# Own step lists for the first units, one more pair of half 0 before half 1, and residual updates moved behind the mixers

## The chip, the cores and the metric

The kernel runs on one core of a Trainium2 chip. The core has five engines with a queue of instructions each: TensorE (PE in the profile) for matrix products and transposes, VectorE (DVE) and GpSimd (POOL) for elementwise work, ScalarE (ACT) for activations and copies, and SyncE (SP), which here only issues DMAs. Each engine works through its own queue in order and waits on semaphores for the others. Matrix results go to PSUM, everything else lies in SBUF. The metric is the device time of one execution in microseconds (us).

## The reference, cut to what matters

There are 1024 tokens (4 sequences of 256) of 512 fp32 values, and two layers of two blocks each. Each block reads a normalised copy of the residual stream and adds its result to it:

```
x = hidden_states                                    # 4 x 256 x 512, fp32
# block 1: retention, 32 query heads, 8 key/value heads, head size 128
y  = layernorm(x)
q, k = rope(y Wq), rope(y Wk);  v = y Wv;  g = y Wg
dt = softplus(y Win + bias);  a = cumsum(-exp(A) * dt)
x += (rmsnorm(causal(exp(a_i - a_j) * q k^T) v) * silu(g)) Wo
# block 2: router, 64 experts, the best 8, and a bias for each expert
# block 3: state space, 128 heads of 64 channels, 8 groups
xs, B, C = silu(conv4(y Wx)), silu(conv4(y WB)), silu(conv4(y WC))
h = causal(exp(a_i - a_j) * C B^T) (dt * xs) + D * xs
x += (rmsnorm per group (h * silu(y Wz))) Wout       # groups of 1024 channels
# block 4: 64 adapters of rank 16, the best 16
```

## The kernel before, in words

**Tiling.** The 1024 tokens are 8 tiles of 128 rows, in two halves of 4 tiles (two sequences each, 512 tokens, the free size of most matmuls). The residual `k.x[t]` stays in SBUF as fp32. An fp32 product is made of three matmuls of split operands: a high part `hi` and the rest `lo`, so hi·hi, lo·hi and hi·lo. Normalised activations lie transposed in `k.xs[half]` as a hi and a lo part. `normalize` (its first part is `moments`, L86: `bn_stats` of each tile) writes them: hi by ACT (L126), lo by DVE (L127).

**Weights.** A weight comes in pieces of 128x1024 (512 KB). `Weights` keeps all pieces in the order of their use. `until(n)` loads every piece up to number n, splits it in `split` (hi is a copy on ACT, L140; lo a subtraction on POOL, L145), and issues the loads of the two pieces after it. A step W calls `step`, which splits the next piece only if its number is at most `due`; `due` is -1 until block 3 runs, so W does nothing in block 1. A piece that nobody asked for earlier is split at its first use. For the numbers in `LATE`, ACT's copy keeps the place it has in the program.

**Order of the work.** Instructions are not sent in the order in which the functions emit them: a scheduler plays the program through on a timeline with its own costs and orders each engine's queue by that. `k.behind(one, made, ...)` adds a dependence without a semaphore's cause in the data: `one` has to be placed behind `made`. The order of emission is written in lists of single letters, one list for each unit of work.

**Block 1** goes through 32 units (key/value head, pair of query heads, half). While unit i is attended, the projections of unit i+1 are emitted: S are the scores q k^T (L408), A the products with v (L420) and the norms, Q the query projection, K the steps of keys and values, G the gate projection, U the silu of the gate, N the norm and the cast to yh (L451) and yl (L452), F and C the output product with Wo (L464) of the unit before, D the decays (`exponents`, up to L303: the row of cumulated sums comes back from DRAM by a broadcast DMA `gb`, is added to the column on DVE and POOL in L299, masked in L303 and goes through exp on ACT). The first unit has the list FIRST1, the others of the first part STEP1. `queries` and `keys` go through `rope` (L355 to L365): two products on DVE, a sum on POOL, a hi copy on ACT and a lo subtraction on DVE (L365).

**Block 2** (router) and the preparation of blocks 3 and 4 are side work, `k.side`: generators from which a step P, T or E takes a piece while the main block goes on.

**Block 3** goes through 64 items: 8 groups of 4 channel pairs, twice, once for each half. For an item, X are the convolution's products and sums (L732), I its inputs, T the transposes (L796), M the mixer (m = decays times C B^T on DVE in L773, the products with it in L821, `xs += skip` in L831 on DVE, the gate in L835 on POOL, yh and yl in L839 and L840), O the output product of the item before (L877) and the sum over the pairs of a group into `acc` (L885), D the decays of the next item. The four settling operations of a group and half, `x += acc * r` (L891, 128x512), follow the output tiles of the group's last pair. `r` is the group's root mean square, of POOL (L863). The order of the items is set by `order`: a first range of pairs of half 0 and then the same pairs of half 1, then each pair for half 0 and half 1 in turn, and a last range of two. A pair that does half 1 straight behind half 0 uses the same split weights; in the first range the weights are loaded and split once for each half. `steps_of` makes the softplus and the cumulated sums of a half before its first item: `ps_v`, a chain of small DVE and ACT operations up to L251, then the products L255 (`ps_cum`), L264 (`ps_in`) and L273 (`ps_tail`).

Of the kernel before, what the change touches and what calls it, by code (L numbers as in the profile page):

```python
# [18 lines left out]
P = 128  # L19
# [8 lines left out]
LONE1, FIRST3, LONE3 = 3, 1, 2  # L28
# [3 lines left out]
LATE = (0, 3)  # L32
FIRST1 = "U S0 S1 S2 K Q0 W Q1 K A0 A1 W K G0 N0 W G1 N1 D E W".split()
STEP1 = "S0 D F S1 S2 K Q0 W Q1 K A0 A1 U W K C W P G0 N0 W G1 N1 E P W".split()
SIDE1 = "S0 D F P S1 S2 T K Q0 P W Q1 T K A0 A1 U W K C P P W G0 P N0 W G1 N1 E P W".split()
STEP3 = "W T0 T1 B I0 W M0 M1 X0 X1 I1 O0 G0 W W O1 W W P O2 W W G1 P W O3 D0 D1 W W".split()
# [3 lines left out]
SIDE3 = "T0 T1 I0 I1 M0 M1 P B X0 X1 P P O0 W O1 G0 G1 W W P O2 O3 W P W P D0 D1 E E".split()  # L40
# [41 lines left out]
def moments(k, tc, t, tag):  # L82

    nc = tc.nc
    stats = k.small([P, 6], f"stats_{tag}_{t}", "ln_stats")
    nc.vector.bn_stats(stats, k.x[t])  # L86
    mv = k.small([P, 2], f"mv_{tag}_{t}", "ln_mv", 6)
    nc.vector.bn_aggr(mv, stats)
    rstd = k.small([P, 1], f"rstd_{tag}_{t}", "ln_rstd", 6)
    nc.gpsimd.tensor_scalar_add(rstd, mv[:, 1:2], EPS)  # L90
    one = nc.gpsimd.tensor_tensor(rstd, rstd, k.neghalf[:, 0:1], ALU.pow)
    if tag == "4" and t == HT - 1:
        k.rooted = one
    return mv[:, 0:1], rstd
# [18 lines left out]
def normalize(k, tc, half, tag, into=("xn",)):  # L113


    nc = tc.nc
    tiles = [HT * half + at for at in range(HT)]
    of = [moments(k, tc, t, tag) for t in tiles]
    ahead = len(into)
    xns = [centre(k, tc, tiles[at], of[at], tag, into[at]) for at in range(ahead)]  # L120
    yield
    for at, t in enumerate(tiles):
        xn = xns[at]
        ps = turned(k, tc, xn, f"xn_{tag}_{t}")
        hi, lo = (part[:, :, at * P:at * P + P] for part in k.xs[half])
        nc.scalar.copy(hi, ps)  # L126
        nc.vector.tensor_tensor(lo, ps, hi.bitcast(F32), ALU.subtract)  # L127
        if at + ahead < HT:
            xns.append(centre(k, tc, tiles[at + ahead], of[at + ahead], tag, into[at % ahead]))
        yield  # L130
# [179 lines left out]
def retention(k, tc, io, arrive, begun, done, tail):  # L310
# [5 lines left out]
    with ExitStack() as st:  # L316
# [35 lines left out]
        def rope(ps, hi, lo, name):  # L352
# [3 lines left out]
            if name == "k_0_0":  # L356

                tc.keep_in_program_order(one)
            t2 = k.wk.tile([P, 2, SEQ], F32, tag="xd", name=f"r2_{name}")
# [5 lines left out]
            nc.vector.tensor_tensor(lo, t1, hi.bitcast(F32), ALU.subtract)  # L365
# [143 lines left out]
        for i in range(-1, len(units) + 1):  # L509
# [50 lines left out]
            def value(z):  # L560
# [9 lines left out]
                W=k.weights.step,  # L570
            )
# [100 lines left out]
def state_space(k, tc, io):  # L672
# [141 lines left out]
    def mixer(p, n):  # L814
# [16 lines left out]
        nc.vector.scalar_tensor_tensor(  # L831
            xs, xs, skip[:, ch:ch + 1], ps_y.rearrange("p t l -> p (t l)"),
            ALU.mult, ALU.add,
        )
        nc.gpsimd.tensor_tensor(xs, xs, p.sg[n], ALU.mult)  # L835
# [29 lines left out]
    def output(p, t):  # L865
# [20 lines left out]
        if p.cp == NC // 2 - 1 and p.g < NG - 1:  # L886
            settle(p, t)

    def settle(p, t):
        xt, a = k.x[HT * p.half + t], acc[p.g, p.half][:, t, :]  # L890
        one = nc.vector.scalar_tensor_tensor(xt, a, p.r[:, t:t + 1], xt, ALU.mult, ALU.add)  # L891
        if (p.g, p.half) == (NG - 1, 0):
            k.behind(one, own.made, "products first")

    cbs, sqs, acc = {}, {}, {}

    pairs, uses = [], []

    order = [range(FIRST3 * NC // 2)]
# [22 lines left out]
    def run(done):  # L922


        with tc.tile_pool(name="s3", bufs=1, reuse_waits="tile") as own.only:
            for i in range(-1, len(pairs) + 1):
# [207 lines left out]
def tile_two_layers(ctx: ExitStack, tc: tile.TileContext, io: dict, out: bass.AP):  # L1134
# [60 lines left out]
    k.hold = k.scaled = k.turned = None  # L1195
    k.const = ctx.enter_context(tc.tile_pool(name="const", bufs=1))
# [112 lines left out]
```

## Time and profile before

| quantity | value |
|---|---|
| median of three runs | 2538.18 us (2537.22 to 2538.46) |
| the profiled execution's own time | 2536.5 us |
| its span, first to last instruction | 2534.7 us |
| PE busy | 2425.6 us (96%), granted clock 0.987 of full speed |
| DVE / POOL / ACT busy | 2062.1 (81%) / 1597.8 (63%) / 1473.0 us (58%) |
| DMA | 206.25 MB, mean 81 GB/s |

Block 1 fills the span up to about 790 us, block 3 begins its products at about 860 us, the decays' steps of its half 1 lie at about 1020 to 1040 us, and the adapters take the last 100 us. In the page, a line of a group names the line of the code, the engine, the operation, output and input, the count, then the busy time and the mean of one, then the engine's idle time just before these instructions and what ended most of it. In a timeline a row has start, duration, engine, line, operation and shape; a bracket at its end is the engine's idle time before it, with the instruction that it waited for. PE's granted clock is 1.00 at full speed.

### The profile page before, as it was taken

To read this page: it belongs to the slowest core of one execution; us is meant where nothing else is said; L and a number is where in the kernel's file an instruction comes from. 1 tells how busy PE (TensorE), PEld (TensorE's weight loads), DVE (VectorE), ACT (ScalarE), POOL (GpSimd) and SP (SyncE) were. 2 spreads that over 40 slices of the span, in tenths; PEclk is the share of its full clock that TensorE was granted. 3 is DMA by queue.
4 is the path that set the end of the run, shared out by engine and by line. 5 is a ranking of instruction groups with operands and counts; after the bars stand their busy time and mean duration, and the time that the engine had idled before them with its cause. 6 is when DMAs were issued, how large, how long until landed. Compare 5 with 4: busy or idle time off the path is not lost.

```text
span 2534.7 us, 36875 instructions
## 1 busy us (share of the span) xinstructions
PE 2425.6 (96%) x14000; PEld 2008.6 (79%) x14000; DVE 2062.1 (81%) x2629; ACT 1473.0 (58%) x2363; POOL 1597.8 (63%) x1123
## 2 busy tenths in 40 slices
PE   7899999999999897899999999999999999999989
PEld 6688888888887775678878888888888888888767
DVE  6577677778888769697988988988988988979973
ACT  3555555556655455465766756666756657657631
POOL 4555546557766547485874865856756855857840
PEclk9899999999999998999999999999999999999999
DMA  3312212213332222332232323222323223323221
GB/s 108 77 58 67 57 44 67 68 50 100 92 92 63 88 77 69 96 117 76 84 92 69 107 67 92 92 76 84 100 67 100 84 67 96 95 69 108 82 90 69
DMA packets 82896, 206.25 MB, mean 81 GB/s; under 512 B 8672, under 2 KB 10592, under 8 KB 82720
## 3 DMA queue, kind: packets, MB, share of 16 engines
q1 hardware_dynamic: 82720, 203.90, 26.5%
q8 instruction: 111, 1.82, 0.3%
q14 instruction: 65, 0.53, 0.1%
HBM read 200.86 MB, written 3.01 MB: 80 GB/s over the span
## 4 chain that ended last, share of the span: by engine, by line
PE 37%; DVE 15%; POOL 6%; issue 4%; ACT 3%; DMA 1%; POOLq 0%; SPq 0%; ACTq 0%; DVEq 0%
PE ps_x L206 9%; PE ps_g L206 8%; PE ps_o L877 8%; DVE m L773 4%; PE ps_y L821 4%; DVE conv L732 3%; PE ps_bc L206 3%; DVE yl L840 2%; PE ps_o L1122 2%; POOL xs L835 1%; DVE m L299 1%; POOL sqs L849 1%; PE ps_t L796 1%; PE ps_h L206 1%; ACT m L1160 1%
## 5 line engine op out<-in xcount | busy, mean ns | idle before, releaser
L206 PE MATMUL ps_g<-xs_hi,wg_h 128*128 128x512 f32 x768 | 306.4, 399 | 2.3 <-ACT wg_h L140 1.7
L773 DVE TENSOR_TENSOR m<-m,cb 128x1536 f32<-128x1536 f32 x128 | 274.7, 2150 | 40.2 <-ACT m L1160 38.8
L206 PE MATMUL ps_g<-xs_lo,wg_h 128*128 128x512 f32 x768 | 300.1, 391 | 0.0
L206 PE MATMUL ps_g<-xs_hi,wg_l 128*128 128x512 f32 x768 | 298.6, 391 | 0.0
L732 DVE SCALAR_TENSOR_TENSOR conv<-ps_x,cw,conv 128x510 f32<-128x510 f32 (+2 forms) x384 | 269.9, 736 | 20.1 <-ACT conv L730 17.5
L1157 ACT ACT_TABLE_LOAD x191 | 245.1, 1283 | 4.1 <-PEq L1297 0.8
L299 POOL TENSOR_TENSOR m<-gb,start 128x512 f32<-128x512 f32 x128 | 151.4, 1185 | 140.6 <-PE ps_y L821 93.0
L877 PE MATMUL ps_o<-wo_h,yh 128*128 128x512 f32 x512 | 213.0, 416 | 20.0 <-DVE acc L885 18.9
L835 POOL TENSOR_TENSOR xs<-xs,sg 128x512 f32<-128x512 f32 x128 | 206.7, 1615 | 38.2 <-DVE xs L831 37.3
L849 POOL TENSOR_TENSOR sqs<-sqs,sq 128x512 f32<-128x512 f32 x112 | 192.9, 1722 | 32.9 <-ACT sq L847 32.9
L362 POOL TENSOR_TENSOR r_q<-r_q,r_q 128x512 f32<-128x512 f32 x64 | 103.3, 1613 | 175.0 <-DVE r_q L361 174.8
L303 POOL TENSOR_SCALAR_AFFINE_SELECT m<-m 128x1024 f32<-128x1024 f32 x160 | 206.0, 1287 | 0.1
L877 PE MATMUL ps_o<-wo_h,yl 128*128 128x512 f32 x512 | 198.2, 401 | 7.8 <-DVE yl L840 7.8
L1160 ACT ACTIVATE xs<-conv,cb 128x512 f32<-128x512 f32 x128 | 90.8, 723 | 193.2 <-DVE conv L732 193.1
L877 PE MATMUL ps_o<-wo_l,yh 128*128 128x512 f32 x512 | 202.7, 396 | 0.0
L206 PE MATMUL ps_x<-xs_lo,wx_h 128*128 128x512 f32 x512 | 202.6, 396 | 0.0
L206 PE MATMUL ps_x<-xs_hi,wx_h 128*128 128x512 f32 x512 | 202.0, 395 | 0.4 <-DVE conv L732 0.2
L206 PE MATMUL ps_x<-xs_hi,wx_l 128*128 128x512 f32 x512 | 201.3, 393 | 0.0
L1160 ACT ACTIVATE m<-m 128x1024 f32<-128x1024 f32 (+1 forms) x160 | 181.5, 1135 | 28.0 <-POOL m L303 28.0
L145 POOL TENSOR_TENSOR wo_l<-raw_wo,wo_h 128x1024 fp32r<-128x1024 f32 x60 | 147.8, 2464 | 79.1 <-ACT wo_h L140 71.8
L145 POOL TENSOR_TENSOR wx_l<-raw_wx,wx_h 128x1024 fp32r<-128x1024 f32 x38 | 96.3, 2534 | 154.3 <-ACT wx_h L140 141.5
L821 PE MATMUL ps_y<-m,xd 128*64 128x128 f32 x2048 | 178.1, 280 | 13.5 <-DVE m L773 9.5
(276 smaller groups left out, 6949.1 us busy)
## 6 DMA issues: line engine op xcount, KB each, us to landing
gb<-cum SPq DMA_DIRECT2D x160, 512.0 KB
raw_wx<-in_L_attn_in_x_dram SPq DMA_DIRECT2D x38, 512.0 KB
raw_wg<-in_L_attn_in_gate_dram SPq DMA_DIRECT2D x38, 512.0 KB
raw_wo<-n_L_attn_out_proj_w_dram SPq DMA_DIRECT2D x38, 512.0 KB
raw_wq<-in_L_attn_Wq_dram SPq DMA_DIRECT2D x22, 512.0 KB
raw_wg<-in_L_attn_Wg_dram SPq DMA_DIRECT2D x22, 512.0 KB
raw_wo<-in_L_attn_Wo_dram SPq DMA_DIRECT2D x22, 512.0 KB
raw_wkv<-in_L_kv_dram SPq DMA_DIRECT2D x11, 512.0 KB
```

What stands on the lines that cost most here:

```text
L145: low = nc.gpsimd.tensor_tensor(lo, w, hi.bitcast(F32), ALU.subtract)
L206: k.line(tc.nc.tensor.matmul(ps, a[:, c, :], b[:, c, :], start=(c == 0 and n == 0), stop=(c == KC - 1 and n == 2)))
L299: one = engine.tensor_tensor(m[:, blk], gb[:, min(blk, 1)], last(at, P), ALU.add)
L303: nc.gpsimd.affine_select(out=causal, in_=causal, compare_op=ALU.is_ge, fill=GONE, base=0, pattern=[[0, 8], [1, P]], channel_multiplier=-1,)
L732: nc.vector.scalar_tensor_tensor(acc[:, :, j:], ps[:, :, :SEQ - j], cw[:, ch, TAPS - 1 - j:TAPS - j], acc[:, :, j:], ALU.mult, ALU.add,)
L773: made = nc.vector.tensor_tensor(mh, mh, cbs[p.g, p.half].rearrange("p z b l -> p z (b l)").unsqueeze(2) .to_broadcast([P, 3, 2, 2 * P]), ...
L821: one = nc.tensor.matmul(ps_y[h * D:h * D + D, 2 * b + z, :], p.xe[:, n, b, h, :] if blk == 2 else xd[:, 2 * b + zs, h, :], m[:, blk, 2 * ...
L835: nc.gpsimd.tensor_tensor(xs, xs, p.sg[n], ALU.mult)
L849: nc.gpsimd.tensor_tensor(total, total, sq, ALU.add)
L877: own.out = nc.tensor.matmul(ps, y[:, at], w[:, n, :], start=(i == 0), stop=(i == 5))
L1157: load = nc.scalar.preload_act_table_set(table)
L1160: ins = nc.scalar.activation(out, in_, func, bias=bias, scale=scale)
```

## The change

- FIRST1 and STEP1 lose their W steps (which do nothing there). Both get a V, STEP1 also V1. V calls `weights.until` with a number: for the first unit (i = 0) that of its Wo piece (3, `wo1_0_0`), for the second (i = 1) 6 with V (`wo1_0_1`) and 7 with V1 (the kv piece of the fifth unit, `wkv1_1_0`), and -1, which asks for nothing, for every other unit. Piece 7 joins LATE.
- `moments`: the `bn_stats` of half 1 in block 1 are placed behind the lo part of the same tile of half 0 (`k.parts`).
- `rope`: the cosine product of the second part of the first keys (`k_0_1`) is placed behind the last lo subtraction that was made, that of the first queries (`k.low`).
- FIRST3 counts pairs instead of groups and goes from 4 pairs (one group) to 5. Half 0 does group 0 and the first pair of group 1, then half 1 the same; from there on the two halves take turns as before. One pair's weights (bc, x, g, o) are loaded and split a second time: 4 loads of 512 KB, 4 ACT copies (L140), 4 POOL subtractions (L145).
- The settling operations leave `output`. `ended`, now called by a step Z at the end of STEP3 and SIDE3 too, puts the four of a group and half into `own.late`; each `mixer` (two in an item) takes two of them behind its own L831. They are placed behind that L831 by `k.behind` (`own.made` is otherwise the newest product of L773). For the last group they are issued in `ended` as before. There are 64 of them before and after.

```
-LONE1, FIRST3, LONE3 = 3, 1, 2
+LONE1, FIRST3, LONE3 = 3, 5, 2
-LATE = (0, 3)
-FIRST1 = "U S0 S1 S2 K Q0 W Q1 K A0 A1 W K G0 N0 W G1 N1 D E W".split()
-STEP1 = "S0 D F S1 S2 K Q0 W Q1 K A0 A1 U W K C W P G0 N0 W G1 N1 E P W".split()
+LATE = (0, 3, 7)
+FIRST1 = "U S0 S1 S2 K Q0 Q1 K A0 A1 K V G0 N0 G1 N1 D E".split()
+STEP1 = "S0 D F S1 S2 K Q0 W Q1 K A0 A1 V U K C P G0 V1 N0 G1 N1 E P".split()
-STEP3 = "... G1 P W O3 D0 D1 W W".split()
+STEP3 = "... G1 P W O3 D0 D1 Z W W".split()
-SIDE3 = "... O2 O3 W P W P D0 D1 E E".split()
+SIDE3 = "... O2 O3 W P W P D0 D1 Z E E".split()
...
 def moments(k, tc, t, tag):
-    nc.vector.bn_stats(stats, k.x[t])
+    one = nc.vector.bn_stats(stats, k.x[t])
+    if tag == "1" and t >= HT:
+        k.behind(one, k.parts[t - HT], "half 0 first")
...
 def normalize(k, tc, half, tag, into=("xn",)):
-        nc.vector.tensor_tensor(lo, ps, hi.bitcast(F32), ALU.subtract)
+        k.parts[t] = nc.vector.tensor_tensor(lo, ps, hi.bitcast(F32), ALU.subtract)
...
     def rope(...):
+            if name == "k_0_1":
+                k.behind(one, k.low, "queries first")
...
-            nc.vector.tensor_tensor(lo, t1, hi.bitcast(F32), ALU.subtract)
+            k.low = nc.vector.tensor_tensor(lo, t1, hi.bitcast(F32), ALU.subtract)
...
+                V=lambda n=0: k.weights.until(u.w.o.n if i == 0 else units[4].w.kv.n - 1 + n if i == 1 else -1),
...
     def mixer(p, n):
-        nc.vector.scalar_tensor_tensor(
+        own.made = nc.vector.scalar_tensor_tensor(
             xs, xs, skip[:, ch:ch + 1], ps_y.rearrange("p t l -> p (t l)"),
             ALU.mult, ALU.add,
         )
+        for late in own.late[0:2]:
+            settle(*late)
+        own.late = own.late[2:]
...
     def output(p, t):
-        if p.cp == NC // 2 - 1 and p.g < NG - 1:
-            settle(p, t)
     def settle(p, t):
-        if (p.g, p.half) == (NG - 1, 0):
+        if (p.g, p.half) != (NG - 1, 1):
             k.behind(one, own.made, "products first")
-    order = [range(FIRST3 * NC // 2)]
+    order = [range(FIRST3)]
...
                 def ended():
-                    if before.half == 1:
+                    if before.cp != NC // 2 - 1:
+                        return
+                    if (before.g, before.half) == (NG - 1, 1):
                         scale(before)
-                    for t in range(HT):
-                        settle(before, t)
-                    k.hold = own.exp if before.half == 0 else None
-                    done(before.half)
+                    own.late += [(before, t) for t in range(HT)]
+                    if before.g == NG - 1:
+                        for late in own.late:
+                            settle(*late)
+                        own.late = []
+                    if ends:
+                        k.hold = own.exp if before.half == 0 else None
+                        done(before.half)
```

More of the change, by code (lines that the diff above doesn't have):

```diff
@@ L31 @@
 BANK1, BANK3 = "o", "x"
-LATE = (0, 3)
-FIRST1 = "U S0 S1 S2 K Q0 W Q1 K A0 A1 W K G0 N0 W G1 N1 D E W".split()
-STEP1 = "S0 D F S1 S2 K Q0 W Q1 K A0 A1 U W K C W P G0 N0 W G1 N1 E P W".split()
+LATE = (0, 3, 7)
+FIRST1 = "U S0 S1 S2 K Q0 Q1 K A0 A1 K V G0 N0 G1 N1 D E".split()
+STEP1 = "S0 D F S1 S2 K Q0 W Q1 K A0 A1 V U K C P G0 V1 N0 G1 N1 E P".split()
 SIDE1 = "S0 D F P S1 S2 T K Q0 P W Q1 T K A0 A1 U W K C P P W G0 P N0 W G1 N1 E P W".split()
-STEP3 = "W T0 T1 B I0 W M0 M1 X0 X1 I1 O0 G0 W W O1 W W P O2 W W G1 P W O3 D0 D1 W W".split()
+STEP3 = "W T0 T1 B I0 W M0 M1 X0 X1 I1 O0 G0 W W O1 W W P O2 W W G1 P W O3 D0 D1 Z W W".split()
 FILL3 = "B X0 X1 I0 I1 P P G0 G1 W W P P W D0 D1 E E".split()
@@ L39 @@
 END3 = "O0 O1 O2 O3 Z P P P".split()
-SIDE3 = "T0 T1 I0 I1 M0 M1 P B X0 X1 P P O0 W O1 G0 G1 W W P O2 O3 W P W P D0 D1 E E".split()
+SIDE3 = "T0 T1 I0 I1 M0 M1 P B X0 X1 P P O0 W O1 G0 G1 W W P O2 O3 W P W P D0 D1 Z E E".split()
 def mid(ap, n):
@@ L945, in ended @@
                 def ended():
-                    if before.half == 1:
+                    if before.cp != NC // 2 - 1:
+                        return
+                    if (before.g, before.half) == (NG - 1, 1):
                         scale(before)
-                    for t in range(HT):
-                        settle(before, t)
-                    k.hold = own.exp if before.half == 0 else None
-                    done(before.half)
+                    own.late += [(before, t) for t in range(HT)]
+                    if before.g == NG - 1:
+                        for late in own.late:
+                            settle(*late)
+                        own.late = []
+                    if ends:
+                        k.hold = own.exp if before.half == 0 else None
+                        done(before.half)
                 step = dict(
@@ L1195, in tile_two_layers @@
     k.hold = k.scaled = k.turned = None
+    k.parts = {}
     k.const = ctx.enter_context(tc.tile_pool(name="const", bufs=1))
```

## The prediction

> **What bounds the kernel now.** I read the busy shares and slices first, then the list of what TensorE waits for, then the timeline around its long waits, stage by stage.
>
> ```profile
> PE 2425.6 (96%) x14000; PEld 2008.6 (79%) x14000; DVE 2062.1 (81%) x2629; ACT 1473.0 (58%) x2363; POOL 1597.8 (63%) x1123
> ...
> PE   7899999999999897899999999999999999999989
> ...
> PEclk9899999999999998999999999999999999999999
> ```
>
> TensorE is busy for 2425.6 of 2534.7 us, so all its idle time is 109 us; nothing that leaves its matmuls alone can gain more than that and what the clock lost. The slices show where it lies: the first two (0 to 127 us), those around 950 to 1100 us, and the end. Between 1300 and 2350 us the timeline's PE waits sum to only 8.9 us.
>
> ```profile
> PE ps_o L877 <- DVE acc L885: 18.9, 20, 5.2
> ...
> PE ps_o L464 <- ACT wo_h L140: 7.5, 1, 7.5
> ...
> PE ps_cum L255 <- DVE e L251: 7.0, 1, 7.0
> ...
> PE ps_sc L408 <- DVE r L448: 4.1, 3, 2.4
> ...
> PE ps_sc L408 <- DVE qs L365: 3.7, 1, 3.7
> ```
>
> The columns are microseconds in all, times, and the longest. Four waits that happen once stand out, and the change touches three of them: wo_h, e and qs. Their places, in the timeline of PE:
>
> ```profile
> 53.62 0.58 PE L408 MATMUL ps_sc<-qs,kh 128*128 128x256 f32 x1 [3.71 <-DVE qs L365]
> ...
> 76.75 0.51 PE L408 MATMUL ps_sc<-qs,kh 128*128 128x256 f32 x2 [2.37 <-DVE r L448]
> ...
> 85.43 1.22 PE L464 MATMUL ps_o<-wo_h,yh 128*128 128x512 f32 x2 [7.54 <-ACT wo_h L140]
> 87.87 0.79 PE L464 MATMUL ps_o<-wo_l,yh 128*128 128x512 f32 x1 [1.22 <-POOL wo_l L145]
> ...
> 1033.12 2.08 PE L255 MATMUL ps_cum<-upper,e 128*128 128x128 f32 x8 [7.03 <-DVE e L251]
> ...
> 1539.91 0.74 PE L877 MATMUL ps_o<-wo_h,yl 128*128 128x512 f32 x2 [0.20 <-DVE yl L840]
> ```
>
> and the other engines at the same places:
>
> ```profile
> 49.49 0.67 DVE L355 TENSOR_TENSOR r_k<-ps_k,room 128x512 f32<-128x512 f32 x1
> ...
> 51.81 1.76 DVE L365 TENSOR_TENSOR qs<-r_q,qs 128x512 fp32r<-128x512 f32 x1
> ...
> 82.96 1.48 ACT L1160 ACTIVATE m<-m 128x1536 f32<-128x1536 f32 x1 [1.06 <-POOL m L303]
> 84.35 1.03 ACT L140 CAST wo_h<-raw_wo 128x1024 fp32r<-128x1024 f32 x1
> ...
> 1544.61 5.91 DVE L891 SCALAR_TENSOR_TENSOR x<-acc,r,x 128x512 f32<-128x512 f32 x4 [1.98 <-POOL r L863]
> ```
>
> The reader should see that the weight's split at 84.35 has no wait of its own: it stood in ACT's queue behind two exps that came late. And that TensorE loses more than the waits: behind each of the three, its matmuls run slower. The 18 score matmuls from 53.62 to 57.21 took 3.59 us; 12 of the same shape from 91.75 to 93.17 took 1.42. Granted clock was 0.83 in 50 to 60, 0.50 in 80 to 90, 0.67 in 1030 to 1040, and 1.00 in 60 to 70 and 1040 to 1050.
>
> **Part 1, start.** At 11.19 PE waits 1.90 us for xs_lo; `bn_stats` of half 1 (0.68 us each, median of its row) stand in front of it on DVE. They go behind. One lies between: -0.6 us (0 to -1.9).
>
> **Part 2, first queries.** The lo of the first queries (51.81, 1.76 us) loses from its front the three products of the key's rope (0.67, 0.69, 0.68, from 49.49 to 51.6). On POOL the queries' sum (47.08) also moves past two additions of 1.02 us each. Still ahead are the first part's lo, up to 49.3, two operations of 0.28 and 0.29, and ACT's hi. I put its end at about 51.3 instead of 53.57: -2.3 us of wait, and 1.4 of 3.71 stays. The slow score matmuls: 18 at the later rate would be 2.13 instead of 3.59, so -1.5. Behind the queries wait now the key's products and, through them, the key's lo; nothing on PE reads those before the next unit. Sum -3.8 (bounds: -1.9, if ACT's hi is next and the clock still drops, to -5.2, the whole wait and the clock).
>
> **Part 3, the first Wo.** V asks for piece 3 before the exps: ACT copies it behind the squares at about 60 us, POOL subtracts (2.36 us) ahead of its additions in L299. Both waits, 7.54 and 1.22, lose their cause. What is late next: DVE now has two additions in L299 (0.69 and 0.87) ahead of the first r of L448, and these wait for the broadcast `gb` until 75.34. So r ends at 77.6 instead of 76.7, the scores start 0.8 us later, the yh casts follow to 78.2, and the output product can begin at 78.4 and take 12 x 0.23 = 2.8 us. After it the second and third scores wait for DVE's first product of L412, now behind two additions to x (0.68 each): about 1 us. Then the queries of the next unit begin near 86 instead of 93.17. -7 us, clock included: eight of the output matmuls ran 0.43 apart instead of 0.23. Bounds: -4.7, if the second yh (81.30 to 81.9 before) and its lo are next, 85.43 - 81.9 + 1.2; and -10.8, both waits and 2 us of clock. On SP the two loads behind piece 3 and, for the second unit, pieces 6 and 7 are issued earlier. They go past `gb`; the DMA share there is 0.21 in 60 to 70 and 0.45 in 70 to 80, so I cost that at nothing; it would cost what `gb` comes later, us for us.
>
> **Part 4, one pair more of half 0.** The order of PE up to `ps_v` of half 1 (about 1020.5) is the same. Then the chain of softplus runs to 1033.07 on DVE and ACT, and PE has 24 gate matmuls (5.5 us) to cover it. With the additional pair it has 24 of `ps_x` and 24 of `ps_g`: 48 x 0.228 = 10.9 us, 5.4 more. DVE gets six convolution operations of 0.74 in return, three of them ahead of L251: 2.2. The wait becomes 7.03 - 5.4 + 2.2 = 3.8. `ps_cum` and `ps_in` took 3.5 us from 1033.12; at the medians of their rows (eight of 0.13 apart, two near 0.4) they are 1.8; I count half of the difference, 0.9. Sum -4.1 (0, if the chain comes later by as much as the cover; -8.7, all of it).
>
> The pair's second weights cost ACT 4 x 1.05 and POOL 4 x 2.40 us and 2.1 MB. POOL stands idle for 14.24 us before 1044.25, and the DMA share there is 0.3: 0 (0 to +5, if two splits stand in front of a mixer's POOL work). The waits of 1072 to 1095 sum to 4.6 us; one settling batch sat there on DVE (1089.97 to 1093.66) and leaves: -1 (-4.6 to +2).
>
> **Part 5, the settling.** 64 operations of 0.74 us stay on DVE. What goes is the time in which DVE stood for r, 22.1 us over 13 batches, and the batch in front of yl, which costs PE 0.20 us a group (1539.91, 1720.77, 1901.62 and so on): -1.4 in all. Two operations, 1.5 us, now stand behind each L831 and ahead of L299 of the next decays. For half 1 this falls where DVE is filled: from 1564 to 1574 it would be 3.0 us longer. The first m product there ended at 1575.80 and PE read it at 1579.93; the second ended at 1581.40, read at 1583.69, a slack of 2.3. So 0.7 us a group could reach PE, 6 groups, +4. DVE stood 2.10 us before 1574.04, which takes some. I take +1 (-1.4 to +4).
>
> **Sum.** -0.6 - 3.8 - 7 - 4.1 - 1 + 1 = -15.5, from the profiled execution's 2536.5 (span 2534.7 and 1.8 outside): 2521.0. The median of the runs shown is 1.7 above that execution, so 2522.7, rounded to 2522.5.
>
> [...] The rows: idle of 3.71, 7.54 and 7.03 us each came with a lower clock in the stretch, idle of 1.90 to 2.37 us did not, or hardly. [...]
>
> **Rivals.** *Something else is next at the head.* For it: `gb` landed at 75.34 and three engines stood for it; against: the chain in front of it starts earlier with part 2. Then parts 1 to 3 give 0 + 1.9 + 4.7 and part 4 and the rest nothing: 2531.6. *The cover of half 1 is eaten.* Six convolution operations on a DVE that was busy 7.79 of 10 us from 1020 to 1030 make L251 as late as PE: part 4 and the -1 go, 2527.8. *Slower: the settling lands on the path.* Place: behind L831, where every m product of L773 waits for an exp (40.2 us of DVE idle before L773, 38.8 for ACT m). If both pairs of operations of a batch delay PE in full, 13 x 3.0 = 39, less the +1 that is in the sum: 2560. It balances the gains at 16.5/13 = 1.3 us a batch and is measurably slower from 1.7. Against it: PE's slack of 2.3 to 4.1 us there. *The hints do not bind*, since neither the list nor the placement was what ordered the queues: no change, 2538. Against it: in the changed kernel's queues Wo's copy does stand ahead of the exps.
>
> **Chances and range.** Forecast (-11 to -22) 0.55, a larger gain 0.05, cover eaten 0.18, something else next 0.10, settling on the path 0.09, hints without effect 0.03. A measurement tells 0.2%, 5 us, from no change. Faster: the first three and half of the fourth, 0.83, less 0.02 from the edges, 0.81; slower 0.08; same 0.11. The range runs from all three head bounds and most of part 4 (2508) to the two small cases and a settling at break-even (2538).
>
> **What would show it.** Right: no PE wait on wo_h near 80 us, the clock at 1.00 in 50 to 60 and 80 to 90, `ps_cum` of half 1 waiting under 4 us, no DVE wait on r L863. Wrong: new PE waits on L412 or `gb` between 75 and 90 of over 4 us, waits on m L773 or yl in each group between 1300 and 2350 that sum to over 9 us, or POOL's weight splits named before 1100.

## The result: 1.76% slower, and the profile after

The changed kernel takes 2581.98 us (2579.63 to 2586.99) against 2538.18, each the median of five runs: the ratio is 1.0176 with a 95% interval of 1.0162 to 1.0190. 2522.5 was forecast, with a range up to 2538. Its profiled execution has a span of 2579.7 us, 45.0 more than before.

Busy shares and slices of the kernel after, from the page:

```profile
PE 2440.1 (95%) x14000; PEld 2012.2 (78%) x14000; DVE 2081.0 (81%) x2629; ACT 1480.6 (57%) x2367; POOL 1611.4 (62%) x1127
...
PE   7999999999999898979999999999999999999889
...
PEclk9999999999999899999999999999999999999989
```

PE's busy time grew by 14.5 us with the same 14,000 matmuls, and its idle time from 109 to 139.6. The slices hide where: the loss is thin and spread. A better ruler is the start of `ps_cb`, the products of C and B, with which half 0 of each group begins (timeline of PE, three groups of the kernel after; groups are counted from 0):

```profile
1328.76 1.50 PE L756 MATMUL ps_cb<-bc,bc 128*128 128x128 f32 x12
...
1515.45 1.50 PE L756 MATMUL ps_cb<-bc,bc 128*128 128x128 f32 x12
...
1702.11 1.50 PE L756 MATMUL ps_cb<-bc,bc 128*128 128x128 f32 x12
```

The first of these rows is that of group 2. The distance between two is a group of both halves: 186.7 us. Before, group 2 began at 1323.75 and group 7 at 2227.89, five groups of 180.8 us on the mean. With the row of group 7 (2262.47 after) the span falls into three parts:

| kernel | start of group 2 | five groups | group 7 to the end | span |
|---|---|---|---|---|
| before | 1323.75 | 904.1 | 306.8 | 2534.7 |
| after | 1328.76 | 933.7 | 317.2 | 2579.7 |

So 45.0 = 5.0 + 29.6 + 10.4. What TensorE waits for (us in all, times, the longest) says on whom. Of the kernel after, the four longest lines of block 3 and two of the head:

```profile
PE ps_y L826 <- DVE m L778: 27.1, 20, 3.7
PE ps_o L885 <- DVE acc L893: 20.6, 16, 4.0
PE ps_x L208 <- DVE conv L737: 12.8, 11, 3.0
PE ps_o L885 <- DVE yl L848: 10.4, 7, 3.4
PE ps_sc L412 <- DVE qs L369: 2.8, 1, 2.8
PE ps_sc L412 <- DVE m L416: 2.7, 2, 1.9
```

(L778 is L773 of before, L885 is L877, L893 is L885, L737 is L732, L848 is L840, L412 is L408, L416 is L412, L369 is L365; in the rows below, L301 is L299, L836 is L831, L843 is L835, L897 is L891, L147 is L145, L208 is L206.) Before, the first four read 9.5, 18.9, 0.2 and 7.8. The lines for `wo_h` (7.5) and for `e` of `ps_cum` (7.0) are gone, that of `qs` fell from 3.7 to 2.8. In their place stand waits in every group of block 3, most of them for VectorE; between 1300 and 2350 us those for m sum to 12.5 us, past the 9 that the prediction named as a sign of being wrong. From 1328.76 on, one group:

```profile
1364.98 0.50 PE L208 MATMUL ps_g<-xs_hi,wg_l 128*128 128x512 f32 x1 [0.35 <-POOL wg_l L147]
...
1402.15 0.50 PE L208 MATMUL ps_x<-xs_hi,wx_h 128*128 128x512 f32 x1 [1.15 <-DVE conv L737]
1407.74 0.44 PE L826 MATMUL ps_y<-m,xd 128*64 128x128 f32 x4 [1.66 <-DVE m L778]
1409.80 0.50 PE L208 MATMUL ps_g<-xs_hi,wg_h 128*128 128x512 f32 x1 [0.53 <-ACT sg L1173]
...
1433.31 0.50 PE L885 MATMUL ps_o<-wo_h,yh 128*128 128x512 f32 x1 [0.94 <-DVE acc L893]
```

With two more further on in the group (0.85 for `acc`, 0.49 for m) the waits sum to 5.96 us, where a group of the kernel before had 1.5. That is 4.5 of the 5.9 us. The rest is no wait: TensorE is busy for 180.7 us of a group instead of 179.3, with the same matmuls and the clock at 1.00; why they take longer was not tried. The three waits between 1402 and 1410 stand right behind the second pair of settling operations of half 1, as VectorE's timeline of the kernel after shows (the first two rows are the pairs of half 0):

```profile
1357.75 3.00 DVE L897 SCALAR_TENSOR_TENSOR x<-acc,r,x 128x512 f32<-128x512 f32 x2
...
1362.59 4.58 DVE L897 SCALAR_TENSOR_TENSOR x<-acc,r,x 128x512 f32<-128x512 f32 x2
...
1388.48 0.74 DVE L836 SCALAR_TENSOR_TENSOR xs<-xs,skip,ps_y 128x512 f32<-128x512 f32 x1
1389.13 2.44 DVE L897 SCALAR_TENSOR_TENSOR x<-acc,r,x 128x512 f32<-128x512 f32 x2
1391.50 0.68 DVE L301 TENSOR_TENSOR m<-gb,start 128x512 f32<-128x512 f32 x1
...
1395.55 0.73 DVE L836 SCALAR_TENSOR_TENSOR xs<-xs,skip,ps_y 128x512 f32<-128x512 f32 x1
1396.20 2.43 DVE L897 SCALAR_TENSOR_TENSOR x<-acc,r,x 128x512 f32<-128x512 f32 x2
1398.56 2.88 DVE L301 TENSOR_TENSOR m<-gb,start 128x512 f32<-128x512 f32 x1
1401.36 0.73 DVE L737 SCALAR_TENSOR_TENSOR conv<-ps_x,cw,conv 128x506 f32<-128x506 f32 x1
...
1405.84 1.76 DVE L778 TENSOR_TENSOR m<-m,cb 128x1536 f32<-128x1536 f32 x1 [1.70 <-ACT m L1173]
```

and GpSimd's at the time of the last pair:

```profile
1396.36 1.73 POOL L843 TENSOR_TENSOR xs<-xs,sg 128x512 f32<-128x512 f32 x1 [1.94 <-DVE xs L836]
1398.05 2.84 POOL L147 TENSOR_TENSOR wg_l<-raw_wg,wg_h 128x1024 fp32r<-128x1024 f32 x1
```

A pair was priced at 1.5 us, and the four of a group take 3.00, 4.58, 2.44 and 2.43. Each stands behind the very L836 that also releases POOL's gate product, and all 28 pairs of this kernel overlap that product. Behind the fourth, the decay's addition L301 meets POOL's weight split and takes 2.88 us instead of the 0.68 behind the other three.

### The profile page after: what moved, and what is told of

It reads as the page before. It is cut to its first block, busy times and chain, and to the rows that moved or that the text cites. A ratio compares the mean times of both kernels' runs of the same rounds, so it can differ in the third digit from the quotient of the medians.

```text
span 2579.7 us, 36845 instructions
## 1 busy us (share of the span) xinstructions
PE 2440.1 (95%) x14000; PEld 2012.2 (78%) x14000; DVE 2081.0 (81%) x2629; ACT 1480.6 (57%) x2367; POOL 1611.4 (62%) x1127
## 4 chain that ended last, share of the span: by engine, by line
PE 29%; DVE 24%; ACT 5%; POOL 4%; issue 3%; DMA 1%; SPq 0%; POOLq 0%; ACTq 0%; DVEq 0%
PE ps_o L885 6%; PE ps_g L208 6%; DVE conv L737 6%; PE ps_x L208 5%; DVE m L778 5%; DVE m L301 3%; PE ps_bc L208 3%; DVE x L897 2%; DVE yl L848 2%; PE ps_y L826 2%; PE ps_o L1135 2%; PE ps_h L208 2%; DVE xs L836 2%; ACT m L1173 2%; ACT L1170 1%
## 5 line engine op out<-in xcount | busy, mean ns | idle before, releaser
L737 DVE SCALAR_TENSOR_TENSOR conv<-ps_x,cw,conv 128x508 f32<-128x508 f32 (+2 forms) x384 | 275.5, 739 | 62.9 <-ACT conv L735 59.3
L208 PE MATMUL ps_g<-xs_hi,wg_h 128*128 128x512 f32 x768 | 308.6, 402 | 3.2 <-ACT sg L1173 3.2
L778 DVE TENSOR_TENSOR m<-m,cb 128x1536 f32<-128x1536 f32 x128 | 261.5, 2048 | 53.7 <-ACT m L1173 53.1
L208 PE MATMUL ps_g<-xs_hi,wg_l 128*128 128x512 f32 x768 | 300.3, 393 | 2.1 <-POOL wg_l L147 2.1
L208 PE MATMUL ps_g<-xs_lo,wg_h 128*128 128x512 f32 x768 | 301.2, 392 | 0.0
L301 POOL TENSOR_TENSOR m<-gb,start 128x512 f32<-128x512 f32 x128 | 155.7, 1219 | 158.7 <-PE ps_y L826 102.0
L843 POOL TENSOR_TENSOR xs<-xs,sg 128x512 f32<-128x512 f32 x128 | 210.2, 1642 | 45.3 <-DVE xs L836 45.3
L885 PE MATMUL ps_o<-wo_h,yh 128*128 128x512 f32 x512 | 214.2, 418 | 24.6 <-DVE acc L893 20.6
L208 PE MATMUL ps_x<-xs_hi,wx_h 128*128 128x512 f32 x512 | 204.1, 399 | 12.9 <-DVE conv L737 12.8
L885 PE MATMUL ps_o<-wo_h,yl 128*128 128x512 f32 x512 | 200.0, 400 | 10.4 <-DVE yl L848 10.4
L826 PE MATMUL ps_y<-m,xd 128*64 128x128 f32 x2048 | 180.8, 281 | 30.5 <-DVE m L778 27.1
L885 PE MATMUL ps_o<-wo_l,yh 128*128 128x512 f32 x512 | 202.8, 396 | 0.0
L208 PE MATMUL ps_x<-xs_lo,wx_h 128*128 128x512 f32 x512 | 202.5, 396 | 0.0
L208 PE MATMUL ps_x<-xs_hi,wx_l 128*128 128x512 f32 x512 | 201.1, 393 | 0.0
L147 POOL TENSOR_TENSOR wx_l<-raw_wx,wx_h 128x1024 fp32r<-128x1024 f32 x39 | 99.1, 2540 | 161.1 <-ACT wx_h L142 161.1
L848 DVE SCALAR_TENSOR_TENSOR yl<-xs,nw,yh 128x512 fp32r<-128x512 f32 x128 | 156.9, 1226 | 30.5 <-ACT yh L847 30.4
```

The lines of the kernel that those rows point to most:

```text
L208: k.line(tc.nc.tensor.matmul(ps, a[:, c, :], b[:, c, :], start=(c == 0 and n == 0), stop=(c == KC - 1 and n == 2)))
L301: one = engine.tensor_tensor(m[:, blk], gb[:, min(blk, 1)], last(at, P), ALU.add)
L737: nc.vector.scalar_tensor_tensor(acc[:, :, j:], ps[:, :, :SEQ - j], cw[:, ch, TAPS - 1 - j:TAPS - j], acc[:, :, j:], ALU.mult, ALU.add,)
L778: made = nc.vector.tensor_tensor(mh, mh, cbs[p.g, p.half].rearrange("p z b l -> p z (b l)").unsqueeze(2) .to_broadcast([P, 3, 2, 2 * P]), ...
L826: one = nc.tensor.matmul(ps_y[h * D:h * D + D, 2 * b + z, :], p.xe[:, n, b, h, :] if blk == 2 else xd[:, 2 * b + zs, h, :], m[:, blk, 2 * ...
L848: nc.vector.scalar_tensor_tensor(yl, xs, w, yh.bitcast(F32), ALU.mult, ALU.subtract)
```

## The experiments

Each run is told with its time against the kernel before, timed beside it (median 2537.1, 2537.0, 2535.8 and 2534.9 us in the first four sets, 2536.03 beside the last run). A ratio with an interval stands where it was timed in rounds; the others are single executions, read by their group distance.

### Which part costs: four kernels

`e1_inline`: everything but the settling (the head and the additional pair).

```
-STEP3 = "... G1 P W O3 D0 D1 Z W W".split()
+STEP3 = "... G1 P W O3 D0 D1 W W".split()
 (SIDE3 likewise; ended, mixer and settle as before)
+        if p.cp == NC // 2 - 1 and p.g < NG - 1:
+            settle(p, t)
```

> The changed kernel with one part undone: the four settling operations of a group follow its output tiles again, as before; the head's parts and the additional pair of half 0 stay. Theory 1 (the settling behind the mixers is the loss: it lengthened a group of block 3 from 180.8 to 186.7 us, 5.9 us times six groups, and the entry and the end besides): the group is back at 180.9 us, and the time is 2538 less the 5.7 us that the head gained, 2532, give or take 4 for the additional pair. Rival (the additional pair shifts the cadence of weights and items, and that lengthens the groups): the group stays at 186 to 187 us and the time near 2575.

`e2_settle`: the settling alone, the same edit the other way round on the kernel before.

> The kernel before with one part alone: settling in pairs behind the mixers. Theory 1: a group takes 186 to 187 us, and the time is 2538 + 45 to 50 = 2583 to 2588, since the head's 5.7 us are missing. Rival (additional pair): a group stays at 181 us and the time within 4 us of 2538.

`e3_head`: the lists with V, piece 7 in LATE, "half 0 first" and "queries first", on the kernel before.

> The kernel before with the head's parts alone: the lists of the first units, piece 7 in LATE, half 0 first, queries first. Both theories: the profile of the changed kernel had the same wait of the fifth output product at 106.62 instead of 112.33, so 5.7 us less, 2532.5, with the groups of block 3 at 180.8 us. If the head's earlier weights changed the cadence of block 3 as well, a group is longer than 181 us and the time above 2538.

`e4_first3`: the additional pair alone.

```
-LONE1, FIRST3, LONE3 = 3, 1, 2
+LONE1, FIRST3, LONE3 = 3, 5, 2
-    order = [range(FIRST3 * NC // 2)]
+    order = [range(FIRST3)]
```

> The kernel before with the additional pair alone (first range of five pairs). Theory 1: no wait of 7.0 us at the cumulated sums of half 1, the groups at 180.8 us, and 2533 to 2538. Rival (additional pair): groups of 186 to 187 us and 2575 to 2585.

| run | time, us | ratio (95%) | group 2 | five groups | rest |
|---|---|---|---|---|---|
| e1_inline | 2536.14 | 0.9996 (0.9987 to 1.0005) | 1321.76 | 904.0 | 310.6 |
| e2_settle | 2585.09 | 1.0189 (1.0173 to 1.0204) | 1330.26 | 934.6 | 317.1 |
| e3_head | 2538.40 | 1.0005 (0.9996 to 1.0015) | 1318.90 | 904.1 | 310.9 |
| e4_first3 | 2542.45 | 1.0022 (1.0010 to 1.0033) | 1322.08 | 904.1 | 313.8 |

The settling alone makes the whole loss: +48 us, against +44 for all parts together. The other parts gain nothing either (`e1_inline`): the head starts group 2 4.9 us earlier and gives 4.1 back at the end, the pair starts it 1.7 earlier and gives back 7.0. So two questions remain: by which mechanism the settling costs six microseconds a group, and where the gains of the head go.

### The settling: whose half, which place

`e7_half0` and `e8_half1`: on `e2_settle`, the dependence on `own.made` only for one half's settling.

```
         one = nc.vector.scalar_tensor_tensor(xt, a, p.r[:, t:t + 1], xt, ALU.mult, ALU.add)
-        if (p.g, p.half) != (NG - 1, 1):
+        if p.half == 0:                                                              # e7_half0
+        if p.half == 1 and p.g < NG - 1 or (p.g, p.half) == (NG - 1, 0):             # e8_half1
             k.behind(one, own.made, "products first")
```

> The kernel before with the settling moved behind the mixers for half 0 alone; half 1 settles without the ordering, as the queues place it. Theory (the loss is that of half 1: its four operations fall between the mixers and the next convolutions and products of decays, with 3.3 us of new waits a group): a group takes 181 to 183 us and the time is 2538 to 2552. Rival (each half's settling costs its share of 5.9 us, by DVE time that runs next to POOL's gate products): about 184 us a group, 2560. If half 0 is the loss: 186 us, 2580.

> The kernel before with the settling moved behind the mixers for half 1 alone. Theory (the loss is that of half 1): 184 to 187 us a group and 2565 to 2585. Rival (each half its share): about 184 us, 2560. If half 0 is the loss: 181 us, 2540.

`e7_half0` took 2578.09 us, its groups 185.4 to 186.6. `e8_half1` took 2565.80, and its groups alternate: 186.2, 181.4, 186.2, 182.0, 186.3. Neither half is the cause by itself, and the two surpluses, 5.0 and 3.6 us a group on the mean, are more than the 6.1 of both together. The alternation is the better find: dear and cheap groups have the same four operations and nearly the same settling on DVE, 9.0 and 8.8 us. In the dear ones L299 took 2.88 us behind the second pair, in the cheap ones 0.68. The order of the queues alternates with them, so this is a hint and no proof. From `e8_half1`, DVE, a dear and a cheap group:

```profile
1398.19 2.44 DVE L892 SCALAR_TENSOR_TENSOR x<-acc,r,x 128x512 f32<-128x512 f32 x2
1400.55 2.88 DVE L299 TENSOR_TENSOR m<-gb,start 128x512 f32<-128x512 f32 x1
...
1581.09 2.44 DVE L892 SCALAR_TENSOR_TENSOR x<-acc,r,x 128x512 f32<-128x512 f32 x2
1583.45 0.68 DVE L299 TENSOR_TENSOR m<-gb,start 128x512 f32<-128x512 f32 x1
```

`e11_decays` and `e14_single` look for a better place, behind the product L773 of the next decays instead of behind L831, and one operation behind each mixer instead of two.

```
     def mixer(p, n):
-        for late in own.late[0:2]:      # e11_decays: these three lines stand at the end of decays
-            settle(*late)
-        own.late = own.late[2:]
+        for late in own.late[0:1]:      # e14_single
+            settle(*late)
+        own.late = own.late[1:]
```

> The kernel of e2 with the pairs of settling operations behind the decays' products (L773) of the next item instead of behind the mixers' sums. There POOL's gate product does not start at the same time and the additions for the decays are done. Theory A: two of them take 1.5 to 2 us, and a group 181 to 183 us. Theory B (any place on DVE that the planner does not choose costs its whole time): a group 184 us or more.

> The kernel of e2 with one settling operation behind a mixer instead of two, so that four mixers (two items of a half) share the four of a group. Theory B1 (DVE time in that place beyond a slack of about 2 us): each place then takes 0.74 to 1.3 us, inside the slack, and a group 181 to 183 us. Theory B2 (the ordering costs): 185 us or more, as there are more ordered places.

`e11_decays`: 2580.44 us, groups 185.7 to 186.1. `e14_single`: 2572.80 us, groups 191.7, then 184.4 three times and 184.7. Spreading them saves some 2.5 us a group from the second group on, the other place about 0.9; neither came to the 181 to 183 us that the theory wanted. In `e11_decays` the pairs collide too, with other work of POOL: in groups 2 to 6, those with nothing beside them on POOL take 1.41 us, the others 2.19 to 4.32, and a group's settling still takes 11.2.

### The settling: work, place or collision

`e10_none` leaves the settling of groups 0 to 6 out, to see what it costs at all. `e9_one_input` and `e13_tiny` keep the place and the hint of `e2_settle` and change the operation: one SBUF tensor as input (the old residual is left out of the sum), and 8 columns instead of 512 (the others are not updated). For all three the scheduler ordered the queues anew, so their group times hold a change of order besides.

```
     def settle(p, t):
         xt, a = k.x[HT * p.half + t], acc[p.g, p.half][:, t, :]
+        if p.g < NG - 1: return                                                      # e10_none
+        if p.g < NG - 1: xt, a = xt[:, 0:8], a[:, 0:8]                               # e13_tiny
+        if p.g < NG - 1: one = nc.vector.tensor_scalar_mul(xt, a, p.r[:, t:t + 1])   # e9_one_input, else as before
```

> The kernel before with the settling of groups 0 to 6 left out altogether, so block 3 adds only its last group to the residual. It measures what the settling costs in the kernel before: if its DVE time is hidden there, a group stays at 180.3 to 180.9 us; if it is not, a group falls below 179.5.

> The kernel of e2 (the settling alone behind the mixers), but each of the 56 settling operations of groups 0 to 6 reads one operand from SBUF instead of two: x = acc * r, so the old residual is left out of the sum. Nothing else is left out. Theory A (what costs is that a two-operand operation and POOL's gate product or weight split run at the same time and hold each other up; two of them took 2.4 to 4.6 us instead of 1.5): two take 1.1 us, and a group 181 to 183 us. Theory B (the place costs, whatever the operation: it delays the additions of the next decays and the convolutions): a group 184 us or more.

> The kernel of e2 (the settling behind the mixers), but each settling operation of groups 0 to 6 works on 8 of the 512 columns; the rest of the residual's update is left out. The ordering, the count and the places in the code stay, the DVE time goes. Theory B1 (the place costs by the DVE time it takes there, 2.4 to 4.6 us a pair): a group falls to 180 to 181.5 us, as without settling (180.0). Theory B2 (the ordering itself costs, since the planner then orders the rest worse): a group stays at 184 us or more.

| run | time, us | a group | settling on DVE, a group | L299 on DVE in all |
|---|---|---|---|---|
| before | 2538.18 | 180.8 | 9.8 | 142.7 |
| e10_none | 2533.63 | 180.0 | 0 | 137.4 |
| e2_settle | 2585.09 | 186.9 | 12.5 | 156.0 |
| e9_one_input | 2562.99 | 185.1 | 10.2 | 134.2 |
| e13_tiny | 2559.15 | 182.7 | 7.0 | 129.3 |

In the kernel before, the settling costs 0.8 us a group against none at all, hardly anything. `e13_tiny`, with 182.7, met neither theory's range. And its eight columns, a sixty-fourth of the work, still take 922 ns on average, though the shortest of them took 211. The group of `e13_tiny` by form, busy time and mean:

```profile
L894 DVE SCALAR_TENSOR_TENSOR x<-acc,r,x 128x8 f32<-128x8 f32 x56 | 49.4, 922 | 0.0
```

An operation's time here can be that of its neighbour. DVE and POOL of `e13_tiny`:

```profile
1540.54 1.48 DVE L894 SCALAR_TENSOR_TENSOR x<-acc,r,x 128x8 f32<-128x8 f32 x2
```

```profile
1540.70 1.29 POOL L838 TENSOR_TENSOR xs<-xs,sg 128x512 f32<-128x512 f32 x1 [0.17 <-DVE xs L831]
```

The pair, which starts 0.16 us ahead of POOL's gate product, ends at 1542.02, and the product at 1541.99. The same product took 1.73 us beside the full pair of the kernel after and 1.29 here: each delays the other. The expectation that one SBUF tensor as input would end the collision fell: `tensor_scalar` took 1304 ns on average, although the 14 shortest of the 56 took 472 to 481.

`e16_psum` takes the collision of the settling away and leaves the rest as it is. The settling of groups 0 to 6 reads the mixer's PSUM tile in place of `acc`, so the residual gets a wrong summand, but the order of all engines' instructions in groups 2 to 6 is that of `e2_settle`. The settling also no longer depends on `acc`; in `e2_settle` it never stood waiting for it.

```
-            settle(*late)
+            settle(*late, ps_y.rearrange("p t l -> p (t l)"))
...
-    def settle(p, t):
+    def settle(p, t, ps=None):
+        a = a if ps is None else ps
```

> The kernel of e2 (the settling behind the mixers), but the settling operations of groups 0 to 6 read the mixer's PSUM tile in place of acc, so the residual gets a wrong summand. Type, columns, count and ordering stay; only one operand comes from SBUF now. An operation on 8 columns (e13) took 0.92 us on the mean there, while L831, which reads PSUM too, always takes 0.73. Theory (DVE operations with two SBUF operands wait out POOL's operation, and this is what makes a pair 2.4 to 4.6 us): a pair takes 1.5 us and a group 182 to 184 us. Rival (the ordering and the place cost, not the collision): pairs of 1.5 us too, but 185.5 to 187 us a group.

It took 2552.61 us, 31.0 less than the 2583.59 of the profiled execution of `e2_settle`; a group takes 182.0 instead of 186.9. The settling by form in the two kernels, first `e2_settle`:

```profile
L892 DVE SCALAR_TENSOR_TENSOR x<-acc,r,x 128x512 f32<-128x512 f32 x64 | 99.6, 1598 | 1.1 <-POOL r L866 1.1
```

then `e16_psum`, and a stretch of its DVE:

```profile
L893 DVE SCALAR_TENSOR_TENSOR x<-ps_y,r,x 128x512 f32<-128x512 f32 x56 | 39.3, 742 | 0.0
```

```profile
1541.96 0.73 DVE L831 SCALAR_TENSOR_TENSOR xs<-xs,skip,ps_y 128x512 f32<-128x512 f32 x1
1542.61 1.40 DVE L893 SCALAR_TENSOR_TENSOR x<-ps_y,r,x 128x512 f32<-128x512 f32 x2
1543.93 1.58 DVE L299 TENSOR_TENSOR m<-gb,start 128x512 f32<-128x512 f32 x1
```

With one operand in PSUM each pair takes 1.40 or 1.41 us whatever POOL does, and the mean is the 742 ns that the prediction used. That is not a faster kind of operation: the median of the kernel before, with both inputs in SBUF, is 742 ns too. L299, which still has both inputs in SBUF, keeps colliding (1.58). So of the 6.1 us that a group of `e2_settle` is longer than one of before, 4.9 are the collision of the settling with POOL's work. The remaining 1.2 (2.0 against no settling at all) are left with the new place and its order.

The Trainium skill, "SBUF — State Buffer", section "SBUF: two separate sides", calls the port pair that VectorE and GpSimd share an exclusive lock: a VectorE operation with two SBUF inputs and a GpSimd operation that reads SBUF exclude one another for a whole instruction, and whichever starts first has it. The runs agree: the pair of 8 columns ends 0.03 us behind POOL's product, and with one PSUM input all 56 operations take 733 to 748 ns. The section "Who interferes with whom" adds that `tensor_scalar` can take both ports in a fast mode, which fits the 1304 ns of `e9_one_input`; no run here shows its mode.

### The head: which part gains

`e5_wo_h0` has the lists and "half 0 first", `e6_wo_q` the lists and "queries first", `e15_wo` the lists alone, `e12_woq_pair` is `e6_wo_q` with the additional pair. All keep the settling of before.

```
-    one = nc.vector.bn_stats(stats, k.x[t])                      # e6_wo_q, e12_woq_pair, e15_wo
-    if tag == "1" and t >= HT:
-        k.behind(one, k.parts[t - HT], "half 0 first")
+    nc.vector.bn_stats(stats, k.x[t])
...
-            if name == "k_0_1":                                  # e5_wo_h0, e15_wo
-                k.behind(one, k.low, "queries first")
```

> The kernel before with two of the head's parts: the lists with V and piece 7 in LATE, and half 0 first; the queries' ordering is left out. Its queues behind the first tenth are those of the kernel before but for a few places, in the adapters all of them, while the kernel with all head's parts had another order in the adapters. Theory (the head's gain is real and was lost by the other order at the end): 4 to 6 us below the kernel before, 2532. Rival (what the head gains is lost by waits behind it in any order): within 2 us of 2537.

> The kernel before with the lists, V and piece 7 in LATE, and queries first; half 0 first is left out. Its queues in block 3 and the adapters are those of the kernel before. Theory (the head's gain is real): 4 to 6 us below, 2532, and about 0.5 us above that if half 0 first is worth anything. Rival: within 2 us of 2537.

> The kernel before with the lists, V and piece 7 in LATE alone. With queries first the same made 10 us. By the profiles the wait for the first queries was 3.7 us before and 1.2 us with the ordering, with the slower matmuls behind it 1.5 us. So 4 us above e6: 2530 to 2532, 5 to 7 us below the kernel before. Rival (the two parts work only together): within 2 us of the kernel before.

> The lists with V and piece 7 in LATE, queries first, and the additional pair of half 0; neither half 0 first nor the settling. Its queues in the adapters are those of the kernel before. The pair alone made block 3 1.7 us earlier by its third group and the end 5 us later, with another order in the adapters. Theory (the pair's loss was the order of the adapters): 2 us below the 2526.6 of e6, so 2522 to 2527. Rival (the second weights or the convolutions cost by themselves): 2530 to 2535.

| run | parts | time, us | ratio (95%) | group 2 | rest |
|---|---|---|---|---|---|
| e15_wo | lists | 2527.88 | 0.9973 (0.9961 to 0.9984) | 1315.96 | 306.3 |
| e6_wo_q | lists, queries | 2526.64 | 0.9959 (0.9944 to 0.9974) | 1314.64 | 305.9 |
| e12_woq_pair | lists, queries, pair | 2525.90 | 0.9961 (0.9948 to 0.9973) | 1313.27 | 306.9 |
| e5_wo_h0 | lists, half 0 | 2534.35 | 0.9988 (0.9978 to 0.9998) | 1321.39 | 306.9 |
| e3_head | lists, half 0, queries | 2538.40 | 1.0005 (0.9996 to 1.0015) | 1318.90 | 310.9 |

The groups take 180.8 or 180.9 in all of them. The gain is that of the lists, 0.27%. "Queries first" on top lies inside the intervals. "Half 0 first" costs: `e3_head` against `e6_wo_q` differs in that alone and, with intervals that don't touch, is 11.8 us longer, 4.3 at group 2 and 5.0 at the end by the profiles (the rest lies between profiled executions and medians). At the entry to half 1 `e3_head` waits 1.53 us for `xs_lo`, which `e6_wo_q` does not, and near the end its adapters come in another order, with waits for the router's `xs_lo` of 3.7 us in all, where `e6_wo_q` has none and the kernel before 0.4. PE's timeline of `e3_head`:

```profile
2454.54 0.66 PE L111 MATMUL ps_xn<-ident,xn 128*128 128x128 f32 x4 [1.02 <-DVE xs_lo L129]
2457.43 0.77 PE L208 MATMUL ps_lg<-xs_hi,wr_parts 128*128 128x512 f32 x1 [2.24 <-DVE xs_lo L129]
```

`e15_wo`, `e6_wo_q` and `e12_woq_pair` beat both kernels; which of the three is fastest, the intervals don't tell.

## Why the prediction was wrong, point by point

**Part 5, the settling: the step that failed.** It put "two operations, 1.5 us" behind each L831, made the stretch from 1564 to 1574 "3.0 us longer", let a slack of 2.3 us swallow most, and came to +1. Measured: +48. The 0.74 us was the median of a row whose mean was 1316 ns, and the batch that the prediction shows itself, four in 5.91 us, is 1.48 each. Many operations of before already collided, in a place where the whole settling cost 0.8 us a group; in the new place every pair overlaps the gate product. By forms, before and after:

```profile
L891 DVE SCALAR_TENSOR_TENSOR x<-acc,r,x 128x512 f32<-128x512 f32 x64 | 81.0, 1316 | 22.1 <-POOL r L863 22.1
...
L299 DVE TENSOR_TENSOR m<-gb,start 128x512 f32<-128x512 f32 x128 | 142.7, 1115 | 5.9 <-DMA gb<-cum 3.2 <-PE ps_y L420 2.7
```

```profile
L897 DVE SCALAR_TENSOR_TENSOR x<-acc,r,x 128x512 f32<-128x512 f32 x64 | 95.6, 1534 | 0.0
...
L301 DVE TENSOR_TENSOR m<-gb,start 128x512 f32<-128x512 f32 x128 | 161.3, 1260 | 6.8 <-DMA gb<-cum 3.4 <-PE ps_y L424 3.4
```

The 22.1 us of standing for r did go, as predicted, but it had cost next to nothing. The two rows grew by 14.6 and 18.6 us. The slower rival had the right place, and its price, 3.0 us a batch, meets what was measured (5.9 a group of two batches); but it came out of the uncollided 1.5 us a pair, so the agreement is partly luck. Its 2560 was still 22 us short: it kept the gains of the other parts, which did not come, and had 9 us for the three batches outside of the five groups, where `e2_settle` lost 16.7. Its chance of 0.09 rested on the slack of 2.3 to 4.1 us, and a pair of 2.4 with an L301 of 2.9 behind it is 3.1 us more than was counted at that point alone.

**Part 3, Wo: right.** Both waits are gone. The transposes of the second unit begin at 98.96 in `e15_wo` against 106.77, 7.8 us earlier, for -7; the medians say 7.0, the interval 4.1 to 9.9. The output product, said to begin at 78.4, began there at 78.93, though its first matmuls still stood 0.43 us apart; the clock from 80 to 90 was 0.92, not 1.00.

**Part 2, queries: the wait moved as predicted, the gain is not shown.** From `e15_wo` to `e6_wo_q` the wait for `qs` falls from 3.72 to 1.21, 2.5 us. The transposes nonetheless begin 1.5 us later, at 100.43. In PE's timeline of `e6_wo_q` stand:

```profile
51.07 0.39 PE L410 MATMUL ps_sc<-qs,kh 128*128 128x256 f32 x1 [1.21 <-DVE qs L367]
...
53.93 0.80 PE L410 MATMUL ps_sc<-qs,kh 128*128 128x256 f32 x2 [1.28 <-DVE m L414]
...
78.22 0.79 PE L410 MATMUL ps_sc<-qs,kh 128*128 128x256 f32 x2 [3.49 <-DVE r L450]
```

The scores now outrun the first product of L412 (1.28 of new wait, the very operation that the prediction expected late only in part 3), r waits 1.0 longer than in `e15_wo` (2.47), and the clock, which was to stay at 1.00 from 50 to 60, was 0.66 there against 0.83. Over the whole kernel the ratios of the two runs lie 3.5 us apart, near the -3.8 of the forecast, but their intervals overlap: neither that nor nothing is ruled out.

**Part 1, start: a shorter wait, and not free.** In the kernel after, the wait for `xs_lo` is 1.84 us against 1.90, but it differs between runs: 1.85 to 3.25 in the kernels without this step, 1.31 to 1.84 in the four with it. So the 0.6 may well have come. The step was priced by its own place only; its cost, 11.8 us by the ratios of `e6_wo_q` and `e3_head` (4 by `e15_wo` and `e5_wo_h0`, inside the intervals), lies mostly a thousand microseconds later, in an order that the scheduler chose anew.

**Part 4, the pair: the wait went, the time did not.** Of the 7.03 us at `ps_cum` the kernel after has 0.33 left, at `ps_in` (3.8 was predicted). Group 2 begins 1.7 earlier in `e4_first3` and 1.4 in `e12_woq_pair` against `e6_wo_q`, not 5: a new wait of 1.8 to 2.3 us for `yh` stands at the first output product of the pair. At the end nothing of it is left (2525.90 against 2526.64) or less than nothing (+5 in `e4_first3`, where the adapters' order changed with it).

**The sum.** Without the settling's +1 the forecast would have been a gain of 16.5 us; `e1_inline` measured 1.0 (from 3.3 faster to 1.3 slower). So without part 5 the sum would have failed too. The head in the kernel after brings its transposes 5.7 us forward (101.05 against 106.77), where parts 1 to 3 said 11.4. Of that 2.0 are left at group 2 with the additional pair and without the settling (1321.76 in `e1_inline`), and the settling of the first groups turns them into 5.0 later.

**What stays open.** How the last 1.2 us a group divide between VectorE's time in that place and the changed order was not tried. Nor was why the stretch from group 7 to the end moves between 305.9 and 313.8 us (`e6_wo_q`, `e4_first3`) with edits that lie far ahead of it; even `e10_none`, which has less work, needs 310.7 there. The scheduler reorders the adapters; that this is the whole cause was only read from the queues.

## What to carry to other kernels

Before you move an elementwise operation, take the mean of its row, not its median, and ask on which engine's release it will start: placed behind the operation that also releases GpSimd, the VectorE pairs with two SBUF inputs met its work in all 28 cases here, while those with a PSUM operand ran at their own length beside it. A stall of an engine that is not the bottleneck may be the cheapest place that its work can have. Where a scheduler orders the queues, price each hint by a run of its own: of five parts here one gained 7 us, one could not be told from nothing, one was nothing or a loss depending on the others, and two lost.

## What the runs showed of the hardware that was not expected

- An operation's length on VectorE can be that of its neighbour: 8 columns took 922 ns on average, 512 columns 742 ns when one operand came from PSUM and 1598 when both came from SBUF beside the same GpSimd work.
- Short waits can be followed by more lost clock than a long one; why, the traces don't show. The single wait of 3.71 us in the kernel before was followed by a granted clock of 0.50 only until about 57 us (0.77 from 56 to 58, 1.00 from 58 to 60). In `e6_wo_q` two waits of 1.21 and 1.28 us, with 1.6 us of matmuls between them, were followed by 0.50 from 54 to 60. The prediction took a rest of 1.4 us to lose no clock, and read its rows as if waits of up to 2.37 us hardly lost any. But in the kernel before the clock was 0.70 from 77 to 78, behind the wait of 2.37 that ended at 76.75 and ahead of the one of 7.54 that began at 77.89. By windows of 2 us, in the columns time, length, PE busy and matmuls, clock, DMA share, GB/s, `e6_wo_q` has:

```profile
52.00:54.00 2.00, 0.71 (x7) 0.80 0.00 0
54.00:56.00 2.00, 2.00 (x9) 0.50 0.00 0
56.00:58.00 2.00, 2.00 (x8) 0.50 0.22 16
58.00:60.00 2.00, 2.00 (x6) 0.50 0.74 254
```
